# A graph layer's TensorE order: small products in two runs instead of four, and row transfers by 31 and 23 instead of 32 and 24

## The chip, the core and the metric

The kernel runs on one core of a Trainium2 chip. The metric is the time of one launch on the device in microseconds. A difference is told against the kernel before, run on the same chip.

## The reference

One message-passing layer of a graph network, 12500 nodes with 32 features, 400000 edges sorted by their target `dst`:

```python
h = jnp.maximum(_layernorm(x, axis=-1), 0.0)
e_feat = jnp.concatenate([h[src], h[dst], edge_attr], axis=-1)   # 96 features an edge
v = jax.nn.relu(e_feat @ W1 + b1) @ W2 + b2                      # 64 hidden, 32 out
x_cand = jax.ops.segment_max(v, dst, num_segments=num_nodes)
x = x + jnp.maximum(x_cand, h[:, -32:])
```

## The kernel before

The 400000 edges lie in four stripes of 100000, and each stripe in chunks of 512 edges: 196 chunks, 128 partitions being four stripes of 32 features. The main loop (L863) takes two chunks in a turn, `c` and `c + 1`; it has 96 turns, and the last four chunks are written out behind it. In a turn several chunks are at different stages, and every engine's order is that in which the code calls its helpers, for the scheduler is off; semaphores keep engines apart. With `a = c + 2` and `b = c + 3`, the parts are:

- **The src rows of h.** Twelve of the 16 columns of a chunk are fetched by POOL with indirect DMAs (`gather`, L176), 128 rows each. Four columns are fetched by TensorE: `tile(c, m)` (L326) multiplies one-hots by a copy of `h` in SBUF, 14 matmuls of 128x128 by 448 columns into one PSUM bank, and VectorE reads the bank (mask L349, maximum L350). In some chunks a fifth tile (`MM`) takes the place of one gather. The one-hots are made by VectorE (`one_hots`, L302) and ScalarE (`one_hots_act`, L315 and L316). VectorE turns the fetched rows into features (`to_features`, L366 and L369).
- **Layer one.** Three products go into the four banks `ph` of a turn: edge features (`edges_into`, which starts the sums), span products (`windows_into`) and src rows (`rows_into`, which ends them), each 16 small matmuls of 32x64. The span products stand for `h[dst]`: since edges are sorted, 512 edges touch few nodes. Rows of `q = h @ W1`'s middle part from the chunk's first node on are loaded by SP (L607) and multiplied by one-hots of the edges' places (`window_hots`, L632 and L633). `relu` (L803) reads `ph` on ScalarE.
- **Layer two.** `second_layer` (L813) is 16 small matmuls of 64x32, into two banks. VectorE's `scan` (L825) takes a running maximum along the edges of a node, `add_b2` (L652) adds the bias on ScalarE.
- **Leaving.** In the next turn `leave_1` transposes the result on TensorE (L660) into two banks, copied by ScalarE (L662) and split by VectorE (`leave_rest`, L668); `leave_2` (L677) picks the last edge of every node with the one-hots of `lasts` (L641), ScalarE copies (L683), VectorE adds (L686), and SP writes the rows of nodes to HBM (L693), one DMA for each chunk and stripe, eight a turn, at an address from a register. Consecutive windows overlap, so each of these writes waits for the one before it.

Tiles, transposes, layer two and `leave_2` share three PSUM banks named `pv`, in rotation: a product waits until the bank of three allocations earlier has been read. TensorE's order in a turn is: src rows, tile(a,1), transposes of the two chunks before, tile(a,2), layer two, tile(a,3), `leave_2`, tile(b,0), edge features of the next turn, tile(b,1), tile(b,2), tile(b,3), maybe the fifth tile, span products of the next turn, and tile(a+2,0).

POOL's gathers are held to points of TensorE's order: `HELD` (L66) names for every second gather of a turn the product that must be done before it is issued, by how many turns earlier and by a short name ('a1' to 'b3' for tiles, 'n0' for the next turn's tile 0, 'ht' for src rows, 'tr' transposes, 'l2' layer two, 'lv' `leave_2`).

`W = 32` is the height of a stripe's window in SBUF, `ROWS = 24` the number of node rows that are written for a chunk and stripe. The broadcast loads `db` and `pb` (L580) copy each stripe's edge data to 32 partitions, 1 MB and 0.5 MB for four chunks.

Of the kernel before, what the change touches and what calls it, by code (L numbers as in the profile page):

```python
# [8 lines left out]
F32 = mybir.dt.float32  # L9
# [5 lines left out]
ALU = mybir.AluOpType  # L15
# [9 lines left out]
P = 128  # L25
# [3 lines left out]
HID = 64  # L29
# [1 line left out]
NP = P * NT  # L31
NS = 4
W = 32
ROWS = 24
SHIFT = 8
C = 512
J = C // P
# [25 lines left out]
LATE = NCH - 8  # L63
PIECE = 2 * A0
GP = 3
HELD = {0: (3, 'b1'), 2: (3, 'b2'), 4: (3, 'b3'), 6: (3, 'n0'), 8: (2, 'ht'), 10: (2, 'a1'), 12: (2, 'tr'), 14: (2, 'a2'), 16: (2, 'l2'), 18: (2, 'a3'), 20: (2, 'lv'), 22: (2, 'b0')}  # L66
SOON = {(3, 0): 'a0', (3, 6): 'a2', (4, 0): 'a3', (4, 6): 'b0', (5, 0): 'b1', (5, 6): 'b2'}
ROUND = 12582912.0
LOW = 1e30
# [12 lines left out]
def gnn_kernel(ctx, tc, x, src, src_mm, src_x, src_t, dst, dst_ext, lo, lo_c, ends_b, edge_attr, weights, w1, w2, b2, out):  # L82
# [243 lines left out]
    def tile(c, m):  # L326

        if c not in MMC or m == MM and c not in MMX:
            return
        if m == 0:  # L330
            mm_rows[c] = early.tile([P, MM, D], F32, name="gm", bufs=4)
        if m < MM:
            hot = [hots[c][:, k, m * P:(m + 1) * P] for k in range(A1)]
            mask, row = masks[c][:, m], mm_rows[c][:, m]
        else:
            _, mask, spaces = extras.pop(c)
            hot = [spaces[k // 2][:, k % 2 * P:(k % 2 + 1) * P] for k in range(A1)]
            row = gh[c][-1][:, SOME - 1]
        po = early_ps.tile([P, C], F32, name="pv", bufs=3)[:, :D * A0]
        for k in range(A1):  # L340
            for part in range(2):
                ins = nc.tensor.matmul(po, hot[k], hs[:, part, k].rearrange("p f a -> p (f a)"),  # L342
                                 start=(k == 0 and part == 0), stop=(k == A1 - 1 and part == 1))
        if m == 0 and c % 2 == 0:
            passes(c // 2 - 2, "n0", ins)
        passes(c // 2 - 1, "ab"[c % 2] + str(m), ins)
        of_group = po.rearrange("p (f a) -> p f a", a=A0)
        one = early.tile([P, D, A0], F32, name="one", bufs=2)
        nc.vector.tensor_tensor(one, of_group, mask[:, None, :].to_broadcast([P, D, A0]), op=ALU.mult)  # L349
        nc.vector.tensor_reduce(row, one, axis=AX.X, op=ALU.max)  # L350
# [204 lines left out]
    with tc.tile_pool(name="edges", bufs=3) as pool, tc.tile_pool(name="edges_ps", bufs=1, space=PSUM) as ps:  # L555
# [4 lines left out]
        bases = {}  # L560
        banks = {}
        fetched = {}
        late_x = {}
        old = src_i[:, MMC.start:LATE - 4].rearrange("p c t -> p (c t)").bitcast(F32)
        late = {}
# [19 lines left out]
        def load(c, queue=nc.scalar):  # L585
            if c % LOAD == 0:
                n = min(LOAD, NCH - c) * C
                if c not in edges:
                    load_edges(c)
                ea = edges.pop(c)  # L590
                db = pool.tile([P, LOAD * C], I32, name="db", bufs=2)
                pb = pool.tile([P, LOAD * C], BF16, name="pb", bufs=2)
                if c:
                    load_wide(db, (dst_ext, 1), c, n, queue)
                    load_wide(pb, (pen_d, 0), c, n, queue)
                wide[c] = db, pb
                for k in range(c, min(c + LOAD, NCH)):
                    loaded[k] = [t[:, (k - c) * C:(k - c + 1) * C] for t in (ea, db, pb)]
            if c % 2 == 0:
                _, base = nc.values_load_multi_w_load_instructions(  # L600
                    lo_i[0:1, c:c + 2], engines=[SP], min_val=0, max_val=N,
                    skip_runtime_bounds_check_because="dst is a node, or N where the host pads")
                for k in range(2):
                    bases[c + k] = base[k * NS:(k + 1) * NS]
                fetched[c // 2] = pool.tile([P, 2, HID], F32, name="qf", bufs=3)
                for s in range(NS):
                    nc.sync.dma_start(fetched[c // 2][s * W:(s + 1) * W], q_two[bass.ds(bases[c][s], W)])  # L607
            windows[c] = bases.pop(c)

        def late_load(c, x, k):  # L610
# [37 lines left out]
        def add_b2(c, sm):  # L648

            n = blocks(c) * P  # L650
            sb = pool.tile([P, C], F32, name="sb", bufs=2)
            nc.scalar.activation(sb[:, :n], sm[:, :n], AF.Identity, bias=b2c)  # L652
            return sb
# [135 lines left out]
        def windows_into(c, ph):  # L789
            of = [ofs.pop(c + x) for x in range(2)]  # L790
            q = fetched.pop(c // 2)
            into_ph(ph, [(q[:, x], of[x]) for x in range(2)], False, False)

        def rows_into(c, ph):
            ht = [hts.pop(c + x).rearrange("p k e -> p (k e)") for x in range(2)]
            passes(c // 2, "ht", into_ph(ph, [(w1a, ht[x]) for x in range(2)], False, True))
# [62 lines left out]
        to_features(3, 0)  # L859
        tile(3, 2)  # L860
        sm = None
        windows_into(0, ph)
        for c in range(0, NCH - 4, 2):  # L863
            a, b = c + 2, c + 3
            rows_into(c, ph)
            if c % LOAD:
                load_edges(c + LOAD // 2 + AHEAD)
# [12 lines left out]
            if c:  # L880
                one_hots(b, 0, 2)
                tile(a, 1)
                to_features(a, 1)
                so = [leave_1(c - 2 + x, sbs[x]) for x in range(2)]
                one_hots_act(b)
                for x in range(2):
                    leave_rest(c - 2 + x, so[x])
                one_hots(b, 2, by_act(b).start)
                mask_of(b)
                if c == LATE + 2:  # L890
                    finish(0)
                tile(a, 2)
                to_features(a, 2)
            else:
                tile(b, 3)
            pv = second_layer(c, hid)
            sms = scan(c, pv, sm)
            sm = sms[-1]
            sbs = [add_b2(c + x, sms[x]) for x in range(2)]
            if c:  # L900
                tile(a, 3)
                leave_2(c - 2, so, last)
                if c > LATE:
                    late_rows_of(c - 2)
            one_hots_act(a + 2)
            load_keys(a + KEYS)
            load_key_x(b + 2)
# [5 lines left out]
            if c:  # L913
                tile(b, 0)
                to_features(b, 0)
            ph = edges_into(c + 2)
            last = [lasts(c + x) for x in range(2)]
            one_hots(a + 2, 0, 2)
            if c == LATE + 2:
# [30 lines left out]
            tile(b, MM)  # L950
            to_features(b, 3)
            to_features(b, J)
            windows_into(c + 2, ph)
            tile(a + 2, 0)
            if a + 2 < NCH - 2:
                to_features(a + 2, 0)
# [6 lines left out]
            if c == (NB - 1) * BLOCK:  # L963
                nc.vector.tensor_scalar(bad[:, :NB, 1], bad[:, :NB, 1], float(ROWS), None, op0=ALU.is_ge)

                own = lo_i.rearrange("p (c x) s -> p c x s", x=2)
                half = NCH // 4
                for k in range(2):
                    r = slice(k * half, (k + 1) * half)
                    gap = early.tile([P, NS * BLOCK, J], F32, name="step", bufs=1).rearrange("p a b -> p (a b)")  # L970
                    gap = gap[0:1, :half * NS].rearrange("p (c s) -> p c s", s=NS)
                    nc.vector.tensor_tensor(gap, own[:, r, 1], own[:, r, 0], op=ALU.subtract)
                    nc.vector.tensor_scalar(gap, gap, float(SHIFT), None, op0=ALU.is_lt)
                    nc.vector.tensor_reduce(bad[0:1, NB + 3, k:k + 1], gap, axis=AX.XY, op=ALU.max)
                    n = half - k
                    nc.vector.tensor_tensor(gap[:, :n], own[:, r.start + 1:r.start + 1 + n, 0], own[:, r.start:r.start + n, 0],
                                            op=ALU.subtract)
                    nc.vector.tensor_scalar(gap[:, :n], gap[:, :n], float(SHIFT + W - 1), None, op0=ALU.is_gt)
                    nc.vector.tensor_reduce(bad[0:1, NB + 4, k:k + 1], gap[:, :n], axis=AX.XY, op=ALU.max)
                near = bad[0:1, NB:NB + 3].rearrange("p a b -> p (a b)")  # L980
                for k, of in enumerate(((NCH - 3, 0), (NCH - 2, LATE))):
                    nc.vector.tensor_tensor(near[:, k * (NS - 1):(k + 1) * (NS - 1)], lo_i[:, of[0], :NS - 1],
                                            lo_i[:, of[1], 1:], op=ALU.subtract)
                nc.vector.tensor_scalar(near, near, float(-W), None, op0=ALU.is_gt)
                worst = pool.tile([P, 1], F32, name="worst", bufs=1)
                nc.vector.tensor_reduce(worst, bad, axis=AX.XY, op=ALU.max)
# [7 lines left out]
        nc.gpsimd.drain()  # L994
        ew = rows_next(late_i)
        late_out(LATE)
        rows_into(c, ph)
        hid = relu(c)
        so = [leave_1(c - 2 + x, sbs[x]) for x in range(2)]
# [178 lines left out]
```

## Time and profile before

| | |
|---|---|
| median of 3 runs | 3606.37 us (3602.39 to 3607.51) |
| profiled execution, own time | 3607.06 us |
| its span, first to last instruction | 3605.3 us |
| mean granted TensorE clock | 0.950 |
| q1 (SP's DMAs) | 72834 packets, 77.57 MB |
| q10 (ScalarE's DMAs) | 29828 packets, 108.01 MB |
| q0 (POOL's gathers) | 74592 packets, 38.29 MB |

A row of the groups shows line, engine, operation, what is written and read, the shape and the count; then busy time and mean duration, and the idle time of that engine just before these instructions with what ended most of it. "remote" stands for a semaphore whose sender the profile did not find. In the order of time a row is start, length, engine, line and, in brackets, the idle time before it. Matmuls are shown from their start; their ends are modelled.

### The profile page before, as it was taken

How to read it: one execution, taken by the hardware profiler on the slowest of the kernel's cores; microseconds unless marked ns; L12 is line 12 of the kernel's file. 1: busy time of each engine (PE TensorE's matmuls, PEld its weight loads, DVE VectorE, ACT ScalarE, POOL GpSimd, SP SyncE). 2: the span in 40 equal slices, each digit the busy share in tenths (PEclk: the TensorE clock that was granted, in tenths of full speed). 3: DMA queues.
4: the chain of work that ended last, by engine and by line, in shares of the span. 5: the costliest groups of instructions: out<-in, count | busy, mean ns of one | idle time of the engine just before them, and what ended most of it. 6: DMA issues, size and time to landing. Idle time of an engine off the chain costs nothing.

```text
span 3605.3 us, 55043 instructions
## 1 busy us (share of the span) xinstructions
PE 3192.1 (89%) x19141; PEld 2474.2 (69%) x19141; DVE 2257.1 (63%) x4237; ACT 1563.0 (43%) x2278; POOL 2211.7 (61%) x2353
## 2 busy tenths in 40 slices
PE   5788999988898989899989888989998988999887
PEld 3466776777676767677777666767776767677765
DVE  6456666666566666666666666666666666666666
ACT  4344434343434444444443444444444444344444
POOL 7566656666656666666566666665666666666664
PEclk8799999999999999999999999999999999999998
DMA  5322222222222222222222222222222222222222
GB/s 180 95 56 62 54 65 57 62 49 63 62 62 53 62 54 71 49 63 56 67 49 62 57 68 52 55 61 58 62 55 65 55 64 52 63 59 61 51 66 65
DMA packets 177537, 227.43 MB, mean 63 GB/s; under 512 B 108261, under 2 KB 149093, under 8 KB 164454
## 3 DMA queue, kind: packets, MB, share of 16 engines
q10 hardware_dynamic: 29828, 108.01, 9.4%
q0 software_dynamic: 74592, 38.29, 7.7%
q1 hardware_dynamic: 72834, 77.57, 7.0%
q8 instruction: 151, 2.47, 0.3%
q14 instruction: 132, 1.08, 0.1%
HBM read 212.23 MB, written 11.46 MB: 62 GB/s over the span
## 4 chain that ended last, share of the span: by engine, by line
PE 78%; issue 9%; DVE 8%; another core or an unknown queue 3%; POOL 1%; DMA 1%; ACT 1%; SPq 0%; POOLq 0%; DVEq 0%; ACTq 0%
PE pv L342 62%; PE ph L778 9%; PE pv L677 3%; PE pv L813 2%; DVE one L349 2%; DVE hot L302 2%; PE pv L660 2%; DVE so L668 1%; DVE sm L825 1%; POOL xg L198 1%; DVE ht L366 1%; POOL gh L182 1%; DMA gh<-h_d,src_i 0%; DVE gm L350 0%
## 5 line engine op out<-in xcount | busy, mean ns | idle before, releaser
L182 POOL DMA_INDIRECT gh<-h_d,src_i x2291 | 2165.3, 945 | 1343.0 <-issue 553.5
L342 PE MATMUL pv<-hs,hot 128*128 128x448 f32 x10752 | 2436.4, 381 | 249.1 <-issue 170.1
L342 PEld LDWEIGHTS pv<-hs,hot 128*128 128x128 f32 x10752 | 2067.5, 197 | 749.6 <-issue 388.9
L349 DVE TENSOR_TENSOR one<-pv,mask 128x448 f32<-128x448 f32 x768 | 473.2, 616 | 993.7 <-remote 370.5
L803 ACT ACTIVATE hid<-ph,wt 128x1024 f32<-128x1024 f32 x196 | 209.4, 1114 | 1156.5 <-PE ph L778 1061.4
L350 DVE TENSOR_REDUCE gm<-one 128x32 f32<-128x448 f32 x768 | 476.3, 620 | 26.4
L302 DVE TENSOR_TENSOR hot<-kb,consts 128x1024 fp32r<-128x1024 f16 (+1 forms) x380 | 454.7, 1197 | 0.0
L316 ACT ACTIVATE hot<-away,ones 128x512 fp32r<-128x512 f32 x582 | 420.6, 723 | 18.9
L315 ACT ACTIVATE away<-kb,key_n 128x512 f32<-128x512 f16 x582 | 412.9, 709 | 0.0
L825 DVE TENSOR_TENSOR_SCAN sm<-pb,sm,pv 128x512 f32<-128x512 bf16 x195 | 246.5, 1264 | 121.6 <-remote 61.5
L652 ACT ACTIVATE sb<-sm,wt 128x512 f32<-128x512 f32 x196 | 141.2, 722 | 390.8 <-DVE sm L825 206.9
L662 ACT ACTIVATE so<-pv 128x512 fp32r<-128x512 f32 x196 | 112.6, 595 | 286.6 <-PE pv L660 159.6
L366 DVE STREAM_TRANSPOSE ht<-gh 128x96 f32<-128x96 f32 x774 | 207.1, 268 | 1.2
L668 DVE TENSOR_TENSOR so<-pv,so 128x512 fp32r<-128x512 f32 x196 | 128.9, 673 | 102.4 <-issue 92.6
L677 PE MATMUL pv<-so,last 128*128 128x256 f32 x768 | 118.9, 301 | 77.8 <-DVE sm L825 66.4
L677 PEld LDWEIGHTS pv<-so,last 128*128 128x128 f32 x768 | 112.3, 207 | 91.8 <-issue 88.4
L813 PE MATMUL pv<-hid,wt 64*32 64x512 f32 x1568 | 148.2, 601 | 16.2 <-issue 10.7
L632 ACT ACTIVATE of<-db,below 128x512 f32<-128x512 int32 x194 | 137.6, 709 | 23.3 <-DMA db<-in_dst_ext 20.1
L778 PE MATMUL ph<-ht,wt 32*64 32x512 f32 x1568 | 136.2, 625 | 12.8 <-issue 6.0
L633 ACT ACTIVATE of<-of,ones 128x512 f32<-128x512 f32 x194 | 140.5, 724 | 6.3
L778 PE MATMUL ph<-of,qf 32*64 32x512 f32 x1552 | 113.9, 622 | 13.2 <-ACT of L633 9.6
L641 DVE TENSOR_TENSOR last<-consts,at 128x512 fp32r<-128x512 f32 x192 | 120.0, 663 | 0.0
(129 smaller groups left out, 1088.1 us busy)
## 6 DMA issues: line engine op xcount, KB each, us to landing
ea<-in_edge_attr SPq DMA_DIRECT2D x49, 1024.0 KB
db<-in_dst_ext ACTq DMA_DIRECT2D x48, 1024.0 KB
gh<-h_d,src_i POOLq DMA_INDIRECT x2291
pb<-pen_d ACTq DMA_DIRECT2D x48, 512.0 KB
kb<-key_d ACTq DMA_DIRECT2D x47, 512.0 KB
top_d<-wo SPq DMA_DIRECT2D x752, 3.0 KB
qf<-q_d SPq DMA_DIRECT2D x392, 16.0 KB
q_d<-qs SPq DMA_DIRECT2D x6, 512.0 KB
```

What stands on the lines that cost most here:

```text
L182: ins = nc.gpsimd.indirect_dma_start(out=parts[-1][:, i, :], out_offset=None, in_=h_d[:, :], in_offset=bass.IndirectOffsetOnAxis(ap=src_i[ ...
L302: nc.vector.tensor_tensor(hot_of(c)[:, start:stop], keys[c][:, None, :].to_broadcast([P, n, MM * P]), key_ps[:, start:stop, None].to_broad ...
L315: nc.scalar.activation(away, keys[c], AF.Square, bias=key_n[:, k:k + 1])
L316: nc.scalar.activation(hot_of(c)[:, k], away, AF.Relu, bias=ones, scale=-1.0)
L342: ins = nc.tensor.matmul(po, hot[k], hs[:, part, k].rearrange("p f a -> p (f a)"), start=(k == 0 and part == 0), stop=(k == A1 - 1 and par ...
L349: nc.vector.tensor_tensor(one, of_group, mask[:, None, :].to_broadcast([P, D, A0]), op=ALU.mult)
L350: nc.vector.tensor_reduce(row, one, axis=AX.X, op=ALU.max)
L366: nc.vector.transpose(ht[:, r].rearrange("p k e -> p (k e)"), gh[c][part][:, :r.stop - r.start].rearrange("p k f -> p (k f)"))
L677: ins = nc.tensor.matmul(pw[:, x % n], last[x][:, j].rearrange("p s w -> p (s w)"), sos[x][0][:, j], start=(j == 0 and x < n), stop=(j == ...
L778: ins = nc.tensor.matmul(ph[s][x * HID:(x + 1) * HID], w[g], e[g], start=start, stop=stop)
L813: ins = nc.tensor.matmul(pv[x][s * D:(s + 1) * D], w2x[g], hid[s][g], start=True, stop=True)
L825: nc.vector.tensor_tensor_scan(found[-1][:, :n], loaded.pop(c + x)[2][:, :n], pv[x][:, :n], -LOW if before is None else before[:, C - 1:C] ...
```

## The change

Three things change together.

1. The order. `windows_into` moves from before tile(a+2,0) to directly before `rows_into`, so that span products and src rows stand side by side. `second_layer` moves from behind tile(a,2) to behind tile(b,0), directly before `edges_into`; `scan` and `add_b2` move along, to behind `edges_into`. The hold 'l2' in `HELD` moves to its new place behind 'b0', and 'a3', 'lv' and 'b0' move up.
2. The q rows of a window: 31 (`NEAR`) instead of 32, into three fixed buffers that are cleared once at the start, since the last row of a stripe's 32 is no longer loaded.
3. The node rows of a write: 23 instead of 24. The check of the spans, which sends odd inputs to a general path, uses the new numbers.

```diff
-ROWS = 24
+ROWS = 23
+NEAR = 31
...
-HELD = {..., 14: (2, 'a2'), 16: (2, 'l2'), 18: (2, 'a3'), 20: (2, 'lv'), 22: (2, 'b0')}
+HELD = {..., 14: (2, 'a2'), 16: (2, 'a3'), 18: (2, 'lv'), 20: (2, 'b0'), 22: (2, 'l2')}
...
+        q_bufs = [pool.tile([P, 2, HID], F32, name=f"qf{k}", bufs=1) for k in range(3)]
+        for of in q_bufs:
+            nc.vector.memset(of, 0.0)
...
-                fetched[c // 2] = pool.tile([P, 2, HID], F32, name="qf", bufs=3)
+                fetched[c // 2] = q_bufs[c // 2 % 3]
                 for s in range(NS):
-                    nc.sync.dma_start(fetched[c // 2][s * W:(s + 1) * W], q_two[bass.ds(bases[c][s], W)])
+                    nc.sync.dma_start(fetched[c // 2][s * W:s * W + NEAR], q_two[bass.ds(bases[c][s], NEAR)])
...
-        windows_into(0, ph)
+        sms = []
         for c in range(0, NCH - 4, 2):
             a, b = c + 2, c + 3
+            windows_into(c, ph)
             rows_into(c, ph)
...
                 tile(a, 2)
                 to_features(a, 2)
-            else:
-                tile(b, 3)
-            pv = second_layer(c, hid)
-            sms = scan(c, pv, sm)
-            sm = sms[-1]
-            sbs = [add_b2(c + x, sms[x]) for x in range(2)]
-            if c:
                 tile(a, 3)
                 leave_2(c - 2, so, last)
...
+            else:
+                tile(b, 3)
             one_hots_act(a + 2)
...
                 tile(b, 0)
                 to_features(b, 0)
+            pv = second_layer(c, hid)
             ph = edges_into(c + 2)
+            sms = scan(c, pv, sm)
+            sm = sms[-1]
+            sbs = [add_b2(c + x, sms[x]) for x in range(2)]
             last = [lasts(c + x) for x in range(2)]
             one_hots(a + 2, 0, 2)
...
-            windows_into(c + 2, ph)
             tile(a + 2, 0)
...
-                    nc.vector.tensor_scalar(gap[:, :n], gap[:, :n], float(SHIFT + W - 1), None, op0=ALU.is_gt)
+                    nc.vector.tensor_scalar(gap[:, :n], gap[:, :n], float(SHIFT + NEAR - 1), None, op0=ALU.is_gt)
...
         late_out(LATE)
+        windows_into(c, ph)
         rows_into(c, ph)
```

More of the change, by code (lines that the diff above doesn't have):

```diff
@@ L65 @@
 GP = 3
-HELD = {0: (3, 'b1'), 2: (3, 'b2'), 4: (3, 'b3'), 6: (3, 'n0'), 8: (2, 'ht'), 10: (2, 'a1'), 12: (2, 'tr'), 14: (2, 'a2'), 16: (2, 'l2'), 18: (2, 'a3'), 20: (2, 'lv'), 22: (2, 'b0')}
+HELD = {0: (3, 'b1'), 2: (3, 'b2'), 4: (3, 'b3'), 6: (3, 'n0'), 8: (2, 'ht'), 10: (2, 'a1'), 12: (2, 'tr'), 14: (2, 'a2'), 16: (2, 'a3'), 18: (2, 'lv'), 20: (2, 'b0'), 22: (2, 'l2')}
 SOON = {(3, 0): 'a0', (3, 6): 'a2', (4, 0): 'a3', (4, 6): 'b0', (5, 0): 'b1', (5, 6): 'b2'}
```

## Prediction

> **What bounds the kernel now.** I read the page's busy shares first, then the groups by line in a stretch without start and end, then the chain of one turn of the main loop, then the engines' order of time around its one large hole. The page and the cores' view:
>
> ```profile
> core 0: 3605.3 us, clock 0.950
> PE 3192.1 (89%) x19141; PEld 2474.2 (69%) x19141; DVE 2257.1 (63%) x4237; ACT 1563.0 (43%) x2278; POOL 2211.7 (61%) x2353
> ```
>
> TensorE is the bound, but a share of 89% hides waits and slow clock. The groups from 1500 to 3000 us (busy, mean ns | idle before them):
>
> ```profile
> L342 PE MATMUL pv<-hs,hot 128*128 128x448 f32 x4632 | 1045.6, 380 | 88.0 <-issue 57.2 <-DVE one L349 29.7
> L182 POOL DMA_INDIRECT gh<-h_d,src_i x974 | 919.4, 944 | 581.4 <-issue 238.4 <-PE pv L342 197.2 <-remote 101.1
> L813 PE MATMUL pv<-hid,wt 64*32 64x512 f32 x656 | 61.9, 601 | 7.4 <-issue 4.7 <-DVE so L668 2.7
> L677 PE MATMUL pv<-so,last 128*128 128x256 f32 x328 | 52.6, 309 | 43.5 <-DVE sm L825 41.6 <-issue 1.9
> ```
>
> L813 runs 16 matmuls in a turn, so 656 are 41 turns: 1500/41 = 36.6 us a turn, and the loop has 96. Idle before L342 and L677 is (88.0 + 43.5)/41 = 3.2 us a turn, 308 us in all; the other matmuls hardly wait. One turn in the chain (start, length):
>
> ```profile
> 1822.55 8.60 PE pv L342 x42
> 1831.15 1.04 PE ph L778 x16
> 1832.19 3.01 PE pv L342 x14
> 1835.20 1.04 PE ph L778 x16
> 1836.25 3.00 PE pv L342 x14
> 1839.25 0.87 PE pv L660 x8
> 1840.13 2.92 PE pv L342 x14
> 1843.05 1.25 PE pv L813 x16
> 1844.30 3.26 issue
> 1847.56 4.47 PE pv L342 x14
> 1852.03 0.95 PE pv L677 x8
> 1852.97 2.81 PE pv L342 x14
> 1855.78 1.04 PE ph L778 x16
> ...
> 1872.28 1.36 PE ph L778 x16
> ```
>
> From the src rows at 1835.20 the order is: tile a1, transposes L660, a2, layer two L813, the hole, a3, node products L677, b0, edge features, b1 to b3, span products, then the next turn's tile 0 (n0). The hole lies between layer two and a3. Tile banks are handed out three in rotation, so a3 needs the bank of a2, two allocations of layer two later; between them only L813's 1.25 us hides a2's readout on VectorE. VectorE, POOL and ScalarE there:
>
> ```profile
> 1846.88 0.62 DVE L349 TENSOR_TENSOR one<-pv,mask 128x448 f32<-128x448 f32 x1 [2.47 <-remote]
> 1847.54 0.62 DVE L350 TENSOR_REDUCE gm<-one 128x32 f32<-128x448 f32 x1
> 1848.07 0.27 DVE L366 STREAM_TRANSPOSE ht<-gh 128x96 f32<-128x96 f32 x1
> 1848.26 2.62 DVE L825 TENSOR_TENSOR_SCAN sm<-pb,sm,pv 128x512 f32<-128x512 bf16 x2
> 1844.22 0.94 POOL L182 DMA_INDIRECT gh<-h_d,src_i  x1 [0.30 <-issue]
> 1847.11 0.94 POOL L182 DMA_INDIRECT gh<-h_d,src_i  x1 [1.95 <-remote]
> 1855.72 0.38 ACT L683 ACTIVATE wo<-pv 128x256 f32<-128x256 f32 x1 [4.08 <-remote]
> ```
>
> VectorE stood idle 2.47 us and read a2 at 1846.88, though the chain has a2 end at 1843.05: TensorE's signal came 3.8 us late. A gather held for a TensorE signal started at 1847.11, so POOL saw it then too. The copy L683 likewise: 1855.72, against 1852.98 for the end of L677, 2.7 us late. TensorE's ends are modelled, but the readers' times are not. So signals that come 0 to 4 us late are a given, and what counts is how much TensorE work lies between a product and the next user of its bank. Behind the hole a3 takes 4.47 instead of 3.00 us, for the clock falls:
>
> ```profile
> 1836.00:1846.00 10.00, 8.30 (x60) 6.34 (x52) 5.76 (x10) 6.78 (x10) 7.03 (x8) 1.00 0.32 90
> 1846.00:1857.00 11.00, 9.44 (x53) 7.80 (x54) 5.98 (x11) 3.22 (x6) 6.60 (x7) 0.84 0.13 33
> ```
>
> The column before the last two is the granted clock: 1.00, then 0.84.
>
> **The change, part by part.** *Merged runs.* Three tiles in a row took 8.60 us, 2.87 each; behind a lone small group a tile takes 3.01 or 3.00, and the group 1.04. A lone group so costs 1.04 + 0.14 = 1.18, and four of them 4.72. At the end of the kernel they already stand side by side (start, span):
>
> ```profile
> 3583.02 1.09 PE L813 MATMUL pv<-hid,wt 64*32 64x512 f32 x14 [0.67 <-DVE so L668]
> 3584.04 1.11 PE L778 MATMUL ph<-ea,wt 32*64 32x512 f32 x16
> 3584.95 1.06 PE L778 MATMUL ph<-kb,qf 32*64 32x512 f32 x16
> 3585.80 1.22 PE L778 MATMUL ph<-ht,wt 32*64 32x512 f32 x16
> ```
>
> Layer two before edge features takes 1.02 (two shapes), span before src rows 0.85 (one shape). After: 0.85 + 1.18 and 1.02 + 1.18, 4.23 in all: **-0.5 us** a turn. This is on the path, and nothing hides it.
>
> *The hole.* Layer two now stands behind a3, L677 and b0. a3 takes a bank of the transposes, whose copies on ScalarE and VectorE have all of a2 to finish in. a2's bank goes to b0, covered by a3 and L677: 2.92 + 0.95 = 3.87, against 3.8 late + 0.62 for L349 = 4.4, which leaves 0.5. Layer two's second bank is that of L677: covered by b0's 2.81 and that 0.5, against 2.7 + 0.38 and as much again for the add L686, so about 0.2 remains. b1 takes b0's bank, covered by 1.02 + 1.04: no wait with a signal on time, 1.3 at 2.7 late; I take 0.4. The scan no longer stands ahead of L677. Of 3.2 us so 1.1 remains: **-2.1 us**. Each of these turns on lateness; bounds are 0 (all of it comes back) and -3.2.
>
> *Clock.* 0.050 of 3605 us is 180 us of lost clock, 1.9 a turn; some half falls on the waits themselves (estimate), which leaves 0.9 on work. a3's excess, 4.47 - 3.00, is of that size. With two thirds of the waits gone: **-0.6 us**, bounds 0 and -0.9.
>
> *VectorE's new queue.* The scans now stand behind b0's readout and ahead of the last-edge masks L641, the one-hots L302, b1's readout and the second one-hots, on which n0 waits. ScalarE's b2 additions follow one-hots and copy that do not need them, and have until the next turn's transposes. Durations of L641 and L302:
>
> ```profile
> 1822.93 1.25 DVE L641 TENSOR_TENSOR last<-consts,at 128x512 fp32r<-128x512 f32 x2
> 1824.10 1.20 DVE L302 TENSOR_TENSOR hot<-kb,consts 128x1024 fp32r<-128x1024 f16 x1
> ```
>
> From b0's end VectorE needs 1.51 (L349, L350, L366) + 2.62 + 1.25 + 1.20 + 1.51 + 1.20 = 9.3 us. TensorE reaches n0 after 1.02 + 1.04 + 3 x 2.87 = 10.7. With layer two's signal on time there is 1.4 us to spare; at 3.8 late the scans start at 4.8, the queue ends at 12.6, and n0 waits 1.9. I take the middle: **+1.0 us**, bounds 0 and 1.9.
>
> *DMAs.* Rows of q by 31 and of nodes by 23 change what SP's queue does, whose eight writes a turn stand one behind the other. The waits, the order of time and the queues (1856 to 1859.8 us, two writes):
>
> ```profile
> SPq L693 <- DVE ht L369: 1063.0, 80, 25.3
> 1818.71 29.30 SPq L693 DMA_DIRECT2D top_d<-wo  x8
> 1856.59 13.28 SPq L693 DMA_DIRECT2D top_d<-wo  x8
> q1 hardware_dynamic: 72, 0.01, 1.3%
> ```
>
> SP waited 1063 us for new rows (the name at the end of such a wait can be wrong): over 96 turns 11 us of slack each. 72 packets took 1.3% of 16 engines for 3.8 us, 11 ns each. On one engine 23 rows are then 0.25 us in line and a q load's 62 pieces 0.7, against next to nothing now: 8 x 0.23 + 4 x 0.64 = 4.4 us a turn. At the new pace the slack is 11.1 - 2.2 = 8.9, so I put the cost at **0**, hidden under SP's wait; if pieces take over 22 ns, that cover is gone. As a gain I count nothing: nobody waits for SP now.
>
> The Trainium skill, "DMA: Bandwidth & Descriptors", section "Why a DMA increments its semaphore by 16 and not by 1", says that such a DMA runs on the largest number of engines up to 16 that divides both sides' outer size, the lowest-numbered ones: 12 for 24 rows, 1 for 23 or 31. The 72 packets agree: twice 24 rows and 12 signals. By that rule all these rows meet the broadcast loads, four stripes on four engines, on one of them, and the change costs what the second rival below says.
>
> *The rest.* The gathers' holds follow the new order of the same twelve points. Three clears of q buffers at the start, and other constants in a check: below 2 us, behind the start's loads.
>
> **Sum.** -0.5 - 2.1 - 0.6 + 1.0 = -2.2 us a turn; 96 turns, -211. The profiled execution took 3607.06 us (span 3605.3), 0.7 above the median: 3396, rounded to **3400**. That pace, 34.4, stays above POOL's floor: 974/41 gathers at 0.94 + 0.30, 29.5 us.
>
> **Rivals.** *The wait only moves.* POOL's two rows show a signal coming out 1.7 us after the gathers paused; a faster TensorE leaves POOL fewer pauses, and signals may be later everywhere. Then only the merged runs remain: 3607 - 46 = 3560. For it speaks that POOL's floor is near, against it the cover, which is two to three times as long.
>
> *SP becomes the bound: slower.* With eight writes in 29.30 instead of 13.28 us where broadcast loads run, rows can be delayed a lot. On one engine the 23 rows queue behind one another, and behind the q loads. Per nanosecond of a piece SP's chain grows 0.4 us a turn; its whole slack, 11.1, is used at 28 ns, and from there the kernel is slower than before. At 32 ns, 12.8 - 11.1 = 1.7 us a turn: 3770. Against it: 11 ns in the one stretch that I could read.
>
> *Layer two's signal holds up VectorE: slower.* Another turn shows it:
>
> ```profile
> 1808.84 5.70 another core or an unknown queue
> ```
>
> There the chain stood 5.70 us before the scan. With that lateness behind b0 the queue ends at 1.0 + 5.7 + 2.62 + 1.25 + 1.20 + 1.51 + 1.20 = 14.5, and n0 waits 3.8; without the clock's gain the sum is -0.5 - 2.1 + 3.8 = +1.2 a turn: 3720. It decides from a lateness of about 4.5 us as the usual case.
>
> **How the numbers follow.** Forecast 0.50, the wait only moves 0.15, both faster by over 0.2%, which is about what a measurement of this kernel can tell from no change. Gains and costs that cancel: 0.05. SP 0.16, signal 0.14: slower 0.30. The forecast's own range: low with all waits and clock back and 0.6 at n0, -3.2 - 0.9 - 0.5 + 0.6 = -4.0, 3223, so 3230; high with half of the waits back, 3500. Since cases of both signs count, the range goes on to 3720, over the first and the last rival; what is left out is the worse part of SP's.
>
> **What would show it.** Right: no idle of 2 us or more between L813 and the tile behind it; L342 and L677 idle some 1 us a turn instead of 3.2; two small groups of 16 matmuls side by side at 0.85 to 1.05; clock over 0.965; turns of about 34.4 us; a short wait at n0 on the one-hots L302. Wrong: n0 waiting 3 us or more; SP's waits for new rows gone and L683 or the span products waiting for DMAs; or the same 3 us idle before b0 or b1.

## The result, and the profile after

The changed kernel took 3617.09 us (median of 20 runs, 3592.52 to 3634.95), the kernel before 3603.28 us beside it (20 runs, 3598.59 to 3612.55): ratio 1.0033 [1.0021, 1.0045], slower by a third of a per cent, against 3400 us forecast. This kernel's time depends on the chip: in the later runs the kernel before took 3636 to 3643 us on some chips and 3026 or 3027 us on others, so each ratio below stands beside the kernel before on its own chip. I call the two kinds held chips and free chips. Four chips took part in the later runs; the one that was used twice was held both times, and no chip was seen as both kinds. The prediction, and the trace behind it, are of a held one.

The profiled execution of the changed kernel took 3608.11 us. Its cores' view, its busy shares, and the groups from 1500 to 3000 us, again 41 turns:

```profile
core 0: 3606.2 us, clock 0.947
PE 3255.3 (90%) x19141; PEld 2503.4 (69%) x19141; DVE 2246.9 (62%) x4240; ACT 1556.7 (43%) x2278; POOL 2216.5 (61%) x2353
L343 PE MATMUL pv<-hs,hot 128*128 128x448 f32 x4640 | 1058.8, 380 | 94.8 <-issue 88.5 <-DVE one L350 1.8 <-DVE sm L829 1.7
L183 POOL DMA_INDIRECT gh<-h_d,src_i x977 | 924.4, 946 | 576.0 <-issue 228.2 <-PE pv L343 146.5 <-remote 133.3
L817 PE MATMUL pv<-hid,wt 64*32 64x512 f32 x656 | 76.3, 613 | 20.2 <-DVE one L350 14.9 <-DVE wo L690 2.8 <-issue 2.5
L681 PE MATMUL pv<-so,last 128*128 128x256 f32 x328 | 45.6, 282 | 0.0
```

L343, L183, L817 and L681 are the lines L342, L182, L813 and L677 of before. The 43.5 us ahead of the node products are gone, as forecast. But the tiles' idle time grew from 88.0 to 94.8 us, nearly all of it now "issue", that is with no wait that the profile knows, and layer two waits 20.2 us after 7.4. In all (94.8 + 20.2)/41 = 2.8 us a turn, against (88.0 + 43.5 + 7.4)/41 = 3.4. This is no gain in time, for TensorE's busy time grew (3255.3 us after 3192.1): counted from the start of one layer two to the next, the 59 turns without a fifth tile took 35.3 us in both traces. And what GpSimd (POOL) waited, its idle time without its own "issue", is (576.0 - 228.2)/41 = 8.5 us a turn, after (581.4 - 238.4)/41 = 8.4.

One turn of the chain of waits, in order of time (start, length, what):

```profile
1506.02 11.82 PE pv L343 x52
1517.84 1.90 PE ph L782 x32
1519.74 3.01 PE pv L343 x14
1522.75 0.87 PE pv L664 x8
1523.62 5.73 PE pv L343 x28
1529.35 0.95 PE pv L681 x8
1530.30 2.82 PE pv L343 x14
1533.12 1.02 PE pv L817 x16
1534.14 1.06 PE ph L782 x15
...
1536.12 0.37 PE pv L343
1536.49 0.37 issue
1536.86 0.44 PE pv L343
1537.31 0.96 issue
1538.27 0.37 PE pv L343
1538.63 0.35 issue
1538.98 0.36 PE pv L343
1539.34 1.05 issue
```

Span products and src rows, 32 matmuls in 1.90 us, and the run of layer two and edge features are there; a2 and a3 follow one another without a hole (5.73 us for 28). The hole has moved behind the merged run, into tile b1, and it has a form that the view of before did not show: the tile's matmuls come one by one, 0.7 or 1.4 us apart, though nothing inside this tile waits for anything (its one-hots were made for tile b0 already). What frees them is seen in the order of time of the same stretch:

```profile
1538.35 0.95 POOL L183 DMA_INDIRECT gh<-h_d,src_i  x1 [0.30 <-issue]
1541.11 5.25 PE L343 MATMUL pv<-hs,hot 128*128 128x448 f32 x14 [0.18 <-issue]
1541.21 2.66 DVE L829 TENSOR_TENSOR_SCAN sm<-pb,sm,pv 128x512 f32<-128x512 bf16 x2 [4.41 <-remote]
1541.49 0.95 POOL L183 DMA_INDIRECT gh<-h_d,src_i  x1 [2.19 <-remote]
```

GpSimd's last gather ended at 1539.30. By its place in the turn the next gather (number 22) is held for layer two of this turn, and VectorE's scan waited for the same products, which layer two had finished at 1534.14. At 1541.11, 1.8 us after the gathers paused, TensorE ran on without gaps, and within 0.4 us both signals had arrived. SyncE was slowed too: in the instruction records three of its small register and semaphore steps, 0.03 us otherwise, took 0.70 us each between 1536.8 and 1539.6 us.

### The profile page after: what moved, and what is told of

The parts are those of the page before. It is cut to its first block, busy times and chain, and to the rows that moved or that the text cites. A ratio compares the mean times of both kernels' runs of the same rounds, so it can differ in the third digit from the quotient of the medians.

```text
span 3606.2 us, 55109 instructions
## 1 busy us (share of the span) xinstructions
PE 3255.3 (90%) x19141; PEld 2503.4 (69%) x19141; DVE 2246.9 (62%) x4240; ACT 1556.7 (43%) x2278; POOL 2216.5 (61%) x2353
## 4 chain that ended last, share of the span: by engine, by line
PE 77%; issue 8%; DVE 7%; another core or an unknown queue 6%; ACT 1%; DMA 1%; DVEq 0%; ACTq 0%; POOL 0%; POOLq 0%; SPq 0%
PE pv L343 60%; PE ph L782 9%; PE pv L817 4%; DVE one L350 2%; PE pv L664 2%; PE pv L681 2%; DVE hot L303 1%; DVE so L672 1%; DVE sm L829 1%; DMA pb<-pen_d 1%; DVE ht L367 1%; PE pp L491 0%; ACT hid L807 0%; ACT away L316 0%
## 5 line engine op out<-in xcount | busy, mean ns | idle before, releaser
L183 POOL DMA_INDIRECT gh<-h_d,src_i x2291 | 2170.7, 947 | 1340.0 <-issue 540.0
L343 PE MATMUL pv<-hs,hot 128*128 128x448 f32 x10752 | 2463.8, 381 | 226.4 <-issue 204.6
L343 PEld LDWEIGHTS pv<-hs,hot 128*128 128x128 f32 x10752 | 2081.4, 197 | 646.7 <-issue 364.8
L817 PE MATMUL pv<-hid,wt 64*32 64x512 f32 x1568 | 183.4, 615 | 51.0 <-DVE one L350 30.0
L687 ACT ACTIVATE wo<-pv 128x256 f32<-128x256 f32 x95 | 36.5, 385 | 383.4 <-remote 201.3
L782 PE MATMUL ph<-ea,wt 32*64 32x512 f32 x1568 | 147.6, 639 | 19.0 <-issue 17.7
L817 PEld LDWEIGHTS pv<-hid,wt 64*32 64x32 f32 x1568 | 28.4, 105 | 148.4 <-DVE wo L690 64.4
```

The lines of the kernel that those rows point to most:

```text
L183: ins = nc.gpsimd.indirect_dma_start(out=parts[-1][:, i, :], out_offset=None, in_=h_d[:, :], in_offset=bass.IndirectOffsetOnAxis(ap=src_i[ ...
L782: ins = nc.tensor.matmul(ph[s][x * HID:(x + 1) * HID], w[g], e[g], start=start, stop=stop)
L817: ins = nc.tensor.matmul(pv[x][s * D:(s + 1) * D], w2x[g], hid[s][g], start=True, stop=True)
```

## The experiments

**The two halves of the change, on a held chip.** The first kernel has the new order and holds, with 32 and 24 rows; the second the old order, with 31 and 23.

```diff
 # order alone: changed kernel with
-ROWS = 23
-NEAR = 31
+ROWS = 24
+NEAR = 32
 # transfers alone: kernel before with
-ROWS = 24
+ROWS = 23
+NEAR = 31
 ... (the q loads and buffers of the change)
```

Expected of the order alone:

> The new order and holds with the old transfers (24 node rows, 32 q rows). Theory A: while POOL issues gathers back to back, TensorE's signals, and behind them its own matmuls, are held up and come out only when POOL pauses; a turn is POOL's 29.6 us of gathers plus the pauses that let TensorE out, whichever order TensorE has. Then this kernel lies within 15 us of the kernel before, with the waits behind the edge features, as in the changed kernel. Theory B: the order does gain by its longer covers, and the transfers on one engine give it back. Then this kernel is faster than before by over 50 us.

Expected of the transfers alone:

> The old order with the new transfers (23 node rows, 31 q rows on one DMA engine). Theory A: SP has slack, so within 15 us of the kernel before. Theory B: the transfers on one engine cost what the order gains, so slower by over 50 us.

Measured, beside 3638.86 us for the kernel before: order alone 3657.92 us, 1.0058 [1.0037, 1.0079]; transfers alone 3627.14 us, 0.9973 [0.9963, 0.9984]. The product of the two ratios, 1.0031, fits the result, 1.0033. Theory B fell in both; theory A's 15 us hold for the transfers (12 us less) and are passed by the order (19 us more). So the loss is the order's, and the transfers by one engine help a little instead of giving something back.

**A quarter fewer gathers, in both orders, on the same chip.**

```diff
         for k in range(0, n, SOME):
+            if k == SOME and FEW and c in MMC:
+                parts.append(parts[0])
+                continue
             parts.append(gathered.tile([P, SOME, D], F32, name="gh"))
```

> The kernel before without the second three of the twelve gathers of a chunk: the columns of the first three are used twice, so h[src] of three columns is another edge's. POOL issues 6 gathers fewer a turn, 7.5 us; TensorE, VectorE and ScalarE do the same work. Theory A: a turn goes from 36.6 us towards TensorE's own 30 to 32 us, so the kernel takes 3050 to 3250 us, and signals come on time. Theory C, that banks and order alone make the waits, with signals late by an amount that has nothing to do with gathers: within 100 us of the kernel before.

> The changed kernel without the second three of the twelve gathers of a chunk, as in before_less (three columns of h[src] are another edge's). Theory A: 2950 to 3150 us, and here, with POOL out of the way, below before_less by the merged runs and longer covers, 50 to 200 us. Theory C: within 100 us of the changed kernel with all gathers, and not below before_less.

With the gathers that are left out, two of the twelve holds of a turn go too. Measured, one run each: 3441.55 us in the old order, 3060.57 us in the new one, with a clock of 0.963 and 0.989. In the new order this is where theory A put it; in the old one it lies between the two theories. The tiles from 1500 to 3000 us, old order and new:

```profile
L346 PE MATMUL pv<-hs,hot 128*128 128x448 f32 x4837 | 1075.4, 377 | 93.4 <-issue 47.7 <-DVE one L353 44.5
L347 PE MATMUL pv<-hs,hot 128*128 128x448 f32 x5496 | 1157.8, 366 | 13.8 <-issue 8.6 <-DVE hot L307 2.6 <-DVE one L354 2.0
```

With 18 gathers a turn the changed order wins 381 us, 4.0 a turn, which is more than the 2.2 that I had forecast. By the starts of the matmuls the old order still spends 3.4 us from layer two to a3 and 4.1 in a3, where 1.02 and 2.92 are the shortest; in the new order layer two to edge features takes 1.03 and no tile more than 3.2 in the mean. So with fewer gathers the new order does remove the hole, as I had counted on, though these two runs do not tell cover from GpSimd's pauses at other points. With 24 gathers, what it wins is lost again.

**Fewer holds; and a chip of the other kind.** If one pause of GpSimd is enough to let TensorE's signals out, one hold a turn in the right place should do better than twelve.

```diff
-HELD = {0: (3, 'b1'), 2: (3, 'b2'), ..., 22: (2, 'l2')}
+HELD = {0: (3, 'ea')}     # one hold, new order ('l2' in the old order)
+HELD = {}                 # no hold
```

Beside them ran the changed kernel with one of the two products in a tile:

```diff
-            for part in range(2):
+            for part in range(1):
```

> The changed kernel, with one hold of the gathers a turn instead of twelve: the first of a turn's 24 gathers waits for the edge-feature products (the second half of the run l2 ea), the other 23 follow without a wait for TensorE. Theory A (while POOL issues gathers back to back, TensorE's signals and then its own matmuls are held up after a run of short products, until some 1.7 us after POOL pauses): POOL now reaches its pause where the run l2 ea stands, so a turn is 24 gathers by 1.24 us and one pause of about 1.8 us, 31.6 us instead of 36: 3617 - 96 x 4.4 = about 3200 (3100 to 3320), b1 and b2 near 2.9 us each. Rival R (gathers slow TensorE by their number, wherever POOL pauses): the same number of gathers, so 3560 to 3660, with the excess at b1 and b2 as before.

> The changed kernel with none of the twelve holds: the gathers wait for free buffers only (VectorE's transposes). Theory A: POOL still runs into waits that TensorE's late signals decide, at places that nobody chose: 3400 to 3650. Rival H (the holds themselves, twelve waits of POOL on TensorE, cost the time): 3100 to 3250.

> The kernel before, with one hold a turn instead of twelve: the first of 24 gathers waits for layer two's products. Theory A: what the gathers did to TensorE goes, the wait behind layer two that stood in before_less (3.4 us at layer two and 4.1 at a3) stays: 3400 to 3480, so the changed order with one hold gains 150 to 350 us over this. Rival R: 3560 to 3660.

> The changed kernel in which every tile runs the products with the high part of h alone: 7 matmuls for 14 (the low part is left out), about 13 us of TensorE's work a turn less. Theory A (the signals are held by gathers and by the runs of short products, which are all still there): POOL's 29.8 us of gathers and its pauses of 3 to 6 us stay, 3250 to 3600. Rival N (it is the number of TensorE's instructions, 399 a turn, that cannot be got rid of beside the gathers): a third fewer, no hold-up any more, and POOL's gathers alone set the turn at 29.8 us: 3000 to 3080.

Measured, one run each: 2968.10, 2967.56, 3025.29 and 2945.76 us. But the kernel before took 3026.97 us there, so none of these times answers its expectation: on this chip there was nothing to take away. What they tell is another thing. With half of the tiles' matmuls it is only 22 us faster than the version with one hold, so something other than TensorE sets a floor near 2946 us: GpSimd's 2291 gathers, which stand in five rows without a pause of 0.6 us in that trace, 2291 x (0.945 + 0.30) = 2852 us by themselves; and TensorE without hindrance needs 2968 in the new order and 3025 in the old one.

**The change itself, on a free chip.**

> The changed kernel itself once more, beside the kernel before. In the last comparison the kernel before took 3027 us where it had taken 3603 and 3639, and no TensorE position had more than its shortest spacing in any kernel. Theory A2 (what holds TensorE up beside POOL's gathers is a condition that one chip has and another has not): where the kernel before takes near 3027 us, the changed order shows its shorter seams alone, 96 x 0.6 = 58 us, so 2960 to 2985, ratio 0.978 to 0.986; where the kernel before takes near 3600, 1.002 to 1.005 again. Rival H (the changed kernel's hold points cost something of their own): over 2990 where the kernel before takes 3027.

> The changed kernel with one hold a turn (the first of 24 gathers waits for the edge-feature products). A2: 2968 +- 5 where the kernel before takes near 3027, the same as the changed kernel with its twelve holds. Where the kernel before takes near 3600: theory A says 3100 to 3320 (one pause of POOL, right behind the run l2 ea), rival R (gathers slow TensorE by their number wherever POOL pauses) 3560 to 3660.

> The kernel before with one hold a turn (the first of 24 gathers waits for layer two). A2: 3025 +- 5 where the kernel before takes near 3027. Where it takes near 3600: A says 3400 to 3480, R 3560 to 3660.

> The transfers alone (q rows by 31, node rows by 23, the old order). Where the kernel before takes near 3027: TensorE is busy all the time, and no transfer is waited for, so within 0.1% of the kernel before. Where it takes near 3600: 0.996 to 0.999 again. If it gains 0.3% or more also at 3027, the transfers shorten something of their own and not the hold-up.

Measured, beside 3025.91 us for the kernel before (21 runs):

| kernel | us | ratio |
|---|---|---|
| the changed kernel | 2966.20 | 0.9808 [0.9795, 0.9822] |
| the same with one hold | 2965.65 | 0.9804 [0.9791, 0.9818] |
| before with one hold | 3025.35 | 0.9999 [0.9990, 1.0008] |
| transfers alone | 3025.20 | 1.0000 [0.9991, 1.0009] |

Here the same change is 1.9% faster: 3025.91 - 2966.20 = 59.7 us, 0.62 a turn, as A2 had put it; rival H fell, and so did a gain of the transfers of their own. The chain of waits of the old order (the kernel with the transfers alone) and of the new one, most of a turn each:

```profile
1500.11 3.01 PE pv L343 x14
1503.12 1.04 PE ph L782 x16
1504.17 3.00 PE pv L343 x14
1507.17 0.87 PE pv L664 x8
1508.05 2.92 PE pv L343 x14
1510.97 1.02 PE pv L817 x16
1511.99 3.01 PE pv L343 x14
1514.99 0.95 PE pv L681 x8
1515.95 2.81 PE pv L343 x14
1518.76 1.04 PE ph L782 x16
```

```profile
1501.56 1.90 PE ph L782 x32
1503.46 3.01 PE pv L343 x14
1506.47 0.87 PE pv L664 x8
1507.34 5.72 PE pv L343 x28
1513.07 0.94 PE pv L681 x8
1514.01 2.81 PE pv L343 x14
1516.82 1.02 PE pv L817 x16
1517.84 1.04 PE ph L782 x16
1518.88 14.20 PE pv L343 x70
```

There is no "issue" and no other engine in either chain. Also in the old order a3 follows layer two at once (1510.97 + 1.02 = 1511.99): the hole from which my prediction started does not exist on this chip, though the bank and the readers are the same. The page of the profile of the changed kernel there, and its gathers from 1500 us on:

```profile
PE 2900.8 (98%) x19141; PEld 2389.4 (81%) x19141; DVE 2243.7 (76%) x4240; ACT 1556.0 (53%) x2278; POOL 2211.5 (75%) x2353
L183 POOL DMA_INDIRECT gh<-h_d,src_i x1132 | 1070.0, 945 | 359.1 <-issue 257.1 <-PE pv L343 34.3 <-DMA gh<-h_d,src_i 24.0
```

A gather takes the same 945 ns, VectorE and GpSimd are busy 2244 and 2212 us, within 0.3% of the first trace of the change, and rows of up to 424 gathers without a pause of 0.6 us are in this trace. Not one of SyncE's small steps took over 0.3 us (337 did in the first trace of the changed kernel).

**One hold and none, on a held chip.**

> The changed kernel with one hold of the gathers a turn (behind the run l2 ea) for twelve, hoped for on a chip on which the kernel before takes near 3600 us. There theory A (TensorE's signals come out about 1.7 us after GpSimd pauses, so one pause in the right place is enough): 3100 to 3320. Rival R (gathers slow TensorE by their number): 3560 to 3660. Where the kernel before takes near 3026: 2966 again, which tells nothing new.

> The changed kernel without any hold. Where the kernel before takes near 3600: A says 3400 to 3700 (GpSimd pauses where buffers happen to come free), H (the holds themselves cost) 3100 to 3250, R 3560 to 3660. Where it takes near 3026: 2966.

> The kernel before with one hold (behind layer two) for twelve. Where the kernel before takes near 3600: A says 3150 to 3450, R 3560 to 3660. Where it takes near 3026: 3025.

Measured, beside 3642.81 us for the kernel before: new order with one hold 4397.42 us, 1.206 [1.200, 1.212]; without holds 4332.90, 1.187 [1.184, 1.191]; old order with one hold 3903.37, 1.072 [1.069, 1.074]. I had expected a gain of 9 to 15% with one hold, and none of the theories allowed for a loss of this size. The rival by number fell, for the number of gathers is the same; and "one pause in the right place is enough" fell with it. With one hold the new order is even 494 us behind the old one. The cores' view and GpSimd's waits with one hold, new order:

```profile
core 0: 4393.2 us, clock 0.853
POOL gh L183 <- DVE ht L367: 1214.6, 235, 9.2
```

With one hold GpSimd stands in long waits for free buffers (235 times, up to 9.2 us), which VectorE's transposes free. In between it gathers in rows of up to twelve. I took TensorE as losing time where two starts of matmuls are over 0.45 us apart, and looked at rows of ten gathers and more between 500 and 3900 us. From the start of such a row TensorE lost these shares of each 2.5 us: 0.00, 0.00, 0.18, 0.38, 0.83, 0.93. For the fourth to the sixth that is 1.0, 2.1 and 2.3 us. Theory L below, for groups of twelve, counts on 0.5, 0.9 and 1.0 us there, which is too little by half; with these figures its sum, 2966 + 2 x 96 x (5.4 + 2), would be some 4390 us (an estimate).

**Groups of four, six and twelve gathers, on a held chip.**

```diff
+HELD = {0: (3, 'ea'), 4: (3, 'b2'), 8: (3, 'n0'), 12: (2, 'a1'), 16: (2, 'a2'), 20: (2, 'lv')}
+HELD = {0: (3, 'ea'), 6: (3, 'b3'), 12: (2, 'a1'), 18: (2, 'a3')}
+HELD = {0: (3, 'ea'), 12: (2, 'a1')}
```

> The changed kernel with a hold ahead of every fourth gather (six a turn, evenly spread: behind ea, b2, n0, a1, a2 and lv) for one ahead of every second. Where the kernel before takes near 3600: theory L (TensorE is held up when a row of gathers goes on past some seven or eight, 9 to 10 us) says rows of four to eight as in the changed kernel, 3500 to 3680. Rival P (each hold is a pause and the time goes by their number, on a line from 12 holds at 1.003 to one at 1.206): 3950 to 4100. Where the kernel before takes near 3026: 2966, TensorE busy all the time.

> The changed kernel with a hold ahead of every sixth gather (four a turn: behind ea, b3, a1 and a3). Where the kernel before takes near 3600: L says rows of six, 7.5 us, still short of the threshold: 3500 to 3750. P says 4150 to 4280. Where it takes near 3026: 2966.

> The changed kernel with a hold ahead of every twelfth gather (two a turn: behind ea and a1). Where the kernel before takes near 3600: L says rows of twelve, 15 us, that lose about 0.5, 0.9 and 1.0 us in their fourth, fifth and sixth 2.5 us and some 2 us behind them, twice a turn: 3900 to 4300. P says 4300 to 4350. Where it takes near 3026: 2966.

Measured, beside 3635.98 us for the kernel before; the twelve holds, the one and none stand beside the kernel before on their own chips, and a row is counted as gathers with under 0.6 us between them:

| holds a turn | us | ratio | gathers in a row, mean |
|---|---|---|---|
| 12 (the change) | 3617.09 | 1.0033 [1.0021, 1.0045] | 4.2 |
| 6 | 3875.64 | 1.0652 [1.0625, 1.0679] | 6.0 |
| 4 | 4389.03 | 1.2052 [1.2013, 1.2091] | 8.8 |
| 2 | 4515.90 | 1.2416 [1.2396, 1.2437] | 6.9 |
| 1 | 4397.42 | 1.206 [1.200, 1.212] | 7.0 |
| 0 | 4332.90 | 1.187 [1.184, 1.191] | 6.9 |

Neither theory met the sizes: groups of four came in between, groups of six and of twelve were slower than by either, and the time does not go on rising towards one hold and none. The trace speaks less against L than the times do. With groups of twelve, the shares lost in long rows are 0.00, 0.00, 0.00, 0.03, 1.00 and 0.99: nothing for 10 us, then all. What failed in L is that rows stay as long as the groups; groups of six made rows of up to 18. What is left is the direction from twelve holds to four. One row of groups of six, in which three groups have run together, in the order of time:

```profile
1511.75 0.95 POOL L183 DMA_INDIRECT gh<-h_d,src_i  x1 [0.30 <-issue]
1512.53 1.01 PE L782 MATMUL ph<-ea,wt 32*64 32x512 f32 x1 [1.82 <-issue]
1516.12 0.62 DVE L350 TENSOR_TENSOR one<-pv,mask 128x448 f32<-128x448 f32 x1 [10.20 <-remote]
1517.99 10.80 PE L343 MATMUL pv<-hs,hot 128*128 128x448 f32 x42
1529.06 0.94 POOL L183 DMA_INDIRECT gh<-h_d,src_i  x1 [16.36 <-PE pv L343]
```

This row lasted from 1490.48 to 1512.69. In it VectorE waited 10.20 us for a tile that was long done; behind its end the signals came out, and TensorE was back at 42 matmuls without a gap at 1517.99. GpSimd then stood 16.36 us, for its next hold lay behind a TensorE that had to catch up.

A second measure takes the sum of gathering over some time in place of one row: the share of the last 10 us in which GpSimd was inside a row, and for each class of it the share of time that TensorE lost as defined above, from 600 to 2900 us:

| kernel | GpSimd under 70% | 70 to 80% | over 80% |
|---|---|---|---|
| before, held | 0.10 | 0.13 | 0.28 |
| the change, held | 0.04 | 0.12 | 0.34 |
| one hold, new order, held | 0.06 | 0.37 | 0.81 |
| groups of six, held | 0.08 | 0.31 | 0.61 |
| a quarter fewer gathers, old order, held | 0.09 | 0.13 | 0.49 |
| a quarter fewer gathers, new order, held | 0.06 | 0.10 | 0.06 |
| the change, free | | | 0.05 |

On the free chip GpSimd was over 80% nearly all the time. A TensorE that stands makes GpSimd pause, which by itself would give the opposite trend. The sixth row does not follow it, and nothing here says why.

## Why the prediction was wrong, point by point

**The term that failed is the hole, -2.1 us a turn; of its bounds the end at 0, "all of it comes back", came true.** Its first half held: a3 takes 2.80 us from start to start instead of 4.72, and L681 has no idle time. What failed is the sentence that signals 0 to 4 us late are a given, so that more work between a product and the next user of its bank is cover. The lateness is no property of a product: on a free chip the same products have none of it, and on a held one it goes with how much GpSimd has gathered just before. From start to start b1 took 5.15 and b2 4.55 us (59 turns without a fifth tile), against 2.91 and 2.80 at the shortest. At layer two and a3 the new order won 3.7 us a turn, and at edge features, b0, b1 and b2 it lost 4.5. That is the last of my signs of a wrong forecast, only that the time is lost inside b1 and b2 rather than ahead of them. That it comes just there because a TensorE that no longer stops behind layer two releases the holds sooner, so that GpSimd runs on to the next run of short products, is my reading and not shown.

One bank was left out of the prediction. b2 takes the bank of layer two's first product, so it waits for the first scan. In 38 of the 59 turns b2's first matmul starts within 0.2 us of that scan's end, and the scan starts 4.7 us in the mean after the edge features' first matmul, 0.5 on a free chip. This wait costs 0.5 us a turn of the 4.0 that b1 and b2 take too long; of the rest some 1.2 go with matmuls 0.25 to 0.45 us apart, as at half clock, and some 2.3 with longer stops inside the tiles.

**POOL's floor of 29.5 us a turn** was the second half of the mistake. On a held chip a turn is 22.5 us of gathers (924.4/41), 5.6 of their own "issue" (228.2/41) and 8.5 of waits, 36.6, in both orders; the runs with fewer holds suggest that the waits belong to the floor there, for with fewer of them TensorE got no further. With six gathers fewer the new order paid 381 us.

**Merged runs, -0.5:** -0.62 on a free chip, and by difference it is the order's (the transfers alone gave 1.0000). On held chips it is there in the seams, 1.90 us for span products and src rows and, at the shortest, 1.02 for layer two, and is eaten by the waits (layer two takes 1.73 in the mean).

**Clock, -0.6:** no gain; 0.947 after 0.950. In that trace as in the prediction's, half clock follows the stops: from 1541 to 1545 us the granted clock is 0.50, and the matmuls start 0.37 us apart for 0.2. Where the stops are missing the clock is 0.994.

**VectorE's new queue, +1.0 at n0:** no wait; n0 takes 2.90 us, 2.89 at the shortest. This term was oversized, and the rival that built on it, layer two's signal holding up VectorE, fell as it was put: the scan did wait 4.41 us for its signal, but TensorE stood in b1 at the same time and so did not reach n0 early. What a late scan costs comes at b2, as said above.

**DMAs, 0:** nearly right. 0.9973 on a held chip, 1.0000 on a free one. The rival in which SyncE becomes the bound fell, since its slack stayed:

```profile
SPq L697 <- DVE ht L367: 916.2, 85, 24.5
SPq L611 <- DMA db<-in_dst_ext: 199.0, 12, 22.8
```

1063.0 us of waits for rows became 916.2, so of 11.1 us of slack a turn 9.5 are left. The eight writes of a turn took 18.53 us in the mean from the first issue to the last before, and 19.86 with the transfers alone, 1.3 more where I had put 8 x 0.23 = 1.8; with the new order too it is 11.35, so the order moved SyncE's chain more than the transfers did. What its rival feared does happen, a q load stuck behind a broadcast for up to 22.8 us, but twelve times in all, and these rows are fetched early. The number of packets agrees exactly with the Trainium skill's rule on how many engines a DMA uses ("DMA: Bandwidth & Descriptors", section "Why a DMA increments its semaphore by 16 and not by 1"): 752 writes with 12 fewer, and 392 loads with 64 + 16 = 80 against 62 + 1 = 63, make 15688, and SP's queue went from 72834 to 57146.

**The rivals.** "The wait only moves" named the mechanism, a faster TensorE that leaves GpSimd fewer pauses, and I gave it 0.15 because cover seemed two to three times as long. It still counted 46 us for the merged runs, which did not arrive. Why the order costs 0.6% on a held chip, and not nothing, stays open: its rows of gathers are shorter (4.2 against 5.0 before), which speaks against the length of a row as the only measure, and GpSimd's share of time inside a row is the same in both (0.77).

## What to carry to other kernels

A wait that ends late though its producer is done has a cause of its own; before counting cover against it, look at what the other engines did just ahead of each late signal, and ask whether a faster engine makes that worse. Holds that look like scheduling can be what keeps a machine from choking: test what they do by taking them away, on more than one chip. A change of order that pays 2% on one chip and costs 0.3% on another has to be judged on both; of the versions tried that compute the whole result none was best on both kinds (the transfers alone on held chips, the changed kernel on free ones).

## What the runs showed of the hardware that was not expected

Beside four of the six sets of runs the kernel before took 3603 to 3643 us, beside two 3026 or 3027, with the same mean duration of a gather (0.945 us) and, within 2%, of every frequent VectorE and ScalarE instruction. Where it was slow, long rows of indirect gathers on GpSimd went with signals of TensorE that came out over 10 us late, with matmuls and SyncE's small steps that advanced one per 0.70 us, and with their release some 2 to 5 us after the last gather of the row. That this goes with the gathers is shown by leaving a quarter of them out (one run each) and by the holds. What links GpSimd's gathers to TensorE and SyncE, and what a free chip lacks or has, no run here shows.
